# Quantised attention and LoRA feed-forward: quantised x transposed by DMA, and the adapters gated for both batches at once

## The chip, the core and the metric

The kernel runs on one core of a Trainium2 chip. The metric is the device time of one execution in microseconds (us), the median of several runs. The engines are TensorE (PE; its weight loads are listed as PEld), VectorE (DVE), ScalarE (ACT), GpSimd (POOL) and SyncE (SP). In this kernel SP only issues DMA transfers; ScalarE issues some as well, on a queue of its own.

## The reference: what is computed

There are two batches of 1024 tokens with 2048 features each. For each batch:

```
q1 = fake_quant(layernorm(x));  q2 = fake_quant(ctx)      # 8 bits, ctx is 2048 x 2048 per batch
x  = x + q1 @ q2
z  = layernorm(x)
x  = x + z @ kernel + bias + lora(z)
```

The LoRA part sees the 2 x 1024 tokens as 8 groups of 256 tokens. Group b has its own adapter, which is a mixture of 16 adapters of rank 32, weighted by row b of `gate`; beside it there is a shared adapter of rank 32:

```
A_eff = einsum('bn,nri->bri', gate, lora_A)      # per group 32 x 2048
B_eff = einsum('bn,nor->bor', gate, lora_B)
delta = (z @ A_eff.T) @ B_eff.T + (z @ A_shared.T) @ B_shared.T
```

Mixing the adapters by `gate` is called gating below. It does not depend on x.

## The kernel before

The work is done batch by batch. A batch has 8 token tiles of 128 tokens, in 4 groups of 256 (index `g`), and 4 blocks of 512 output columns (index `n`).

**Attention stage.** `prep_x(b, m)` makes one tile of quantised x. VectorE computes statistics (L283 and the small operations after it). ScalarE quantises the tile to 8 bits (L295) and then converts each half of it to bf16 in the buffer `qh` (L298). There is one `qh` for both halves of a tile, and the next tile uses it again; the 8-bit buffer `q8` alternates between two. TensorE transposes the eight 128x128 blocks of a half into PSUM (`pt`, L303), and VectorE copies them to `c1T` (L304), the operand of the attention matmuls.

`quantise` does the same for ctx in pieces of 512 KB: ScalarE writes 16-bit integers (L314) to one of three `q2b` buffers, and VectorE clips and centres them (L317). `column_term` sums the columns of one block of quantised ctx (`pcp` and `pc`). `xattn_pair(b, n, g)` opens the accumulator on ScalarE (L359), runs 2 x 16 matmuls (`pa`, L361), and adds the result to `y` on VectorE (L370).

**Gating.** `load_next` streams ctx and the raw adapters, in an order written out by hand in `todo`, into ten `lit` buffers by DMAs on the SP queue. `gated` multiplies a 256-row slice of raw adapters at a time with `gmat`, a 128 x 32 matrix of gates for the 4 groups of one batch. Four such matmuls fill the four 32-row strips of one PSUM tile (`pg_a` or `pg_b`, L383), which VectorE copies to a `q2b` buffer (L395). For A, `lora_a_step` transposes that tile on TensorE (`pga`, L403) and VectorE sorts it into `acat` (L406). For B, `lora_b_step` writes it to DRAM in eight small DMAs on SP (`bd`, L416), from where `Delta` loads it later. All of it is done once per batch: four A steps and four B steps, set between the attention pairs.

**Feed-forward stage.** `prep_z` normalises and transposes `y` (`ptz`), stores it to DRAM (`zs`) and `lora_ax` applies `acat` (`px`). Then `ffn` runs a two-level Strassen scheme in f32: 7 outer by 7 inner products (L611), with the sums of operands on VectorE and GpSimd (L551, L560), the results added to `y` (L629), and the delta of the adapters slipped in (`pl`, L483). During the last outer product of batch 0, `meanwhile` already prepares batch 1: ctx is quantised and tiles 0 to 3 go through `prep_x`.

The Tile framework places the instructions of each engine in a static order by priorities and dependencies; each engine and each DMA queue then works through its own order and waits where a semaphore tells it to. A DMA also waits for the DMA that used the same completion semaphore before it, and there are eight of these for the SP and ScalarE queues together.

Of the kernel before, what the change touches and what calls it, by code (L numbers as in the profile page):

```python
# [10 lines left out]
F32 = mybir.dt.float32  # L11
# [9 lines left out]
P = 128  # L21
# [45 lines left out]
def tile_quant_xattn_then_lora_ffn(  # L67
# [30 lines left out]
    H = D // 2  # L98
    KH = KT // 2
    KQ = KT // 4  # L100
    GP = GPB * RC

    const = ctx.enter_context(tc.tile_pool(name="const", bufs=1))
    small = ctx.enter_context(tc.tile_pool(name="small", bufs=4))
# [18 lines left out]
    gmat = const.tile([P, 2, GPB // 2, RC], F32, tag="gmat", name="gmat")  # L123
# [7 lines left out]
    ]  # L131


    bd = [dram.tile([GPB, 2, R, D], F32, tag=f"bd{b}", name=f"bd{b}") for b in range(B)]

    def bf(t, n):

# [18 lines left out]
    for b in range(B):  # L156
        for n in range(2):
            todo.extend((b, raw_src(b, n, r)) for r in range(KT // 2))
        for n in range(2, 4):
            for r in range(KT // 2):  # L160
                todo.append((b, raw_src(b, n, r)))
                if r in ((3, 7) if n == 2 else (5, 7)):
                    todo.extend((b, ad_src(la, 2 * (n - 2) + r // 6 if n == 3 else r // 4, h)) for h in range(2))
        for n in range(NN):
            todo.extend((b, ad_src(lb, n, h)) for h in range(2))
    loaded = deque()
    ahead = [2]
# [48 lines left out]

    ident = const.tile([P, P], F32, tag="ident", name="ident")
    make_identity(nc, ident)
    ident_h = const.tile([P, P], BF16, tag="ident_h", name="ident_h")
    nc.gpsimd.tensor_copy(ident_h, ident)  # L220
    ones_h = const.tile([P, P], BF16, tag="ones_h", name="ones_h")
    nc.gpsimd.memset(ones_h, 1.0)

# [22 lines left out]
    for b in range(B):  # L246
        for i in range(2):
            nc.vector.tensor_reduce(
                gval[:, ds(b * GPB + i * 2, 2)], gate_b[:, b * GPB + i : (b + 1) * GPB : 2, :], AX.X, ALU.add
            )  # L250

    def norm_stats(stats, name):
# [22 lines left out]
    def prep_x(b, m, c1T, wk):  # L277

        nm = f"{b}_{m}"
        g, tok = m // MG, ds((m % MG) * P, P)  # L280
        ym = y[g][:, m % MG, :]
        for n in range(NN):
            nc.vector.bn_stats(st1[:, m, n, :], ym[:, ds(n * NB, NB)])  # L283
        mean, rstd = norm_stats(st1[:, m], f"a{nm}")

        k = small.tile([P, 1], F32, tag="kx", name=f"kx_{nm}")
        nc.vector.tensor_mul(k, rstd, inv1)
        o = small.tile([P, 1], F32, tag="ox", name=f"ox_{nm}")
# [6 lines left out]
        nc.scalar.activation(q8, ym, AF.Identity, bias=o, scale=k)  # L295
        rsum = small.tile([P, 2], F32, tag="rsum", name=f"rsum_{nm}")
        for h in range(2):
            nc.scalar.activation(  # L298
                qh[:, ds(h * H, H)], q8[:, ds(h * H, H)], AF.Identity, bias=n_centre, accum_out=rsum[:, h : h + 1]
            )  # L300
            pt = ps_m.tile([P, KH, P], BF16, tag="pm", name=f"pt_{nm}_{h}")
            for kt in range(KH):
                nc.tensor.transpose(pt[:, kt, :], qh[:, ds(h * H + kt * P, P)], ident_h)  # L303
            nc.vector.tensor_copy(c1T[g][:, ds(h * KH, KH), tok], pt)  # L304
# [18 lines left out]

    colt = {}
    pairs = []

    def column_term(b, n, c2):

# [21 lines left out]
    def xattn_pair(b, n, g, c1T, c2):  # L350

        cols = ds(n * NB, NB)
        pairs.append((b, n, g))
        pa = ps_acc.tile([P, MG, NB], F32, tag=("acc0", "acc1", "delta")[len(pairs) % 3], name=f"pa_{b}_{n}_{g}")
        for j in range(MG):

            m = g * MG + j
            with tc.high_priority():
                nc.scalar.activation(pa[:, j, :], colt[n], AF.Identity, bias=r_s[:, m : m + 1])  # L359
            for k in range(KT):  # L360
                nc.tensor.matmul(  # L361
                    pa[:, j, :],
                    c1T[g][:, k, ds(j * P, P)],
                    c2[k // 8][:, k % 8, :],
                    start=False,
                    stop=(k == KT - 1),
                    skip_group_check=True,
                )
        yp = y[g][:, :, cols]
# [6 lines left out]
    def gated(nm):  # L376

        ps = ps_m.tile([P, NB], F32, tag="pm", name=f"pg_{nm}")
        for h in range(2):
            buf, t = next_loaded()  # L380
            for c in range(2):
                row = (2 * h + c) * GP
                nc.tensor.matmul(  # L383
                    ps[row : row + GP, :],
                    gmat.rearrange("p i a r -> p (i a r)"),
                    t[:, c, :],
                    start=True,
                    stop=True,
                    skip_group_check=True,
                )  # L390
            lit.give(buf)
            load_next()
# [3 lines left out]
        return st, sf  # L396

    def lora_a_step(b, n):

        st, sf = gated(f"a{b}_{n}")  # L400
        pt = ps_m.tile([P, KQ, P], F32, tag="pm", name=f"pga_{b}_{n}")
        for k in range(KQ):
            nc.tensor.transpose(pt[:, k, :], sf[:, ds(k * P, P)], ident)  # L403
        q2b.give(st)
        for g in range(GPB):
            nc.vector.tensor_copy(  # L406
                acat[:, ds(n * KQ, KQ), own_col[g], :].rearrange("p k (c r) -> p k c r", c=NC),
                pt.rearrange("p k (c i a r) -> p i a k c r", c=NC, i=2, r=RC)[:, g % 2, g // 2],
            )

    def lora_b_step(b, n):

        st, sf = gated(f"b{b}_{n}")
        for c in range(NC):
            for i in range(2):
                nc.sync.dma_start(  # L416
                    out=bd[b][i::2, i, ds(c * RC, RC), ds(n * NB, NB)],
                    in_=sf[ds(c * GP + i * (GP // 2), GP // 2), :],
                )
        q2b.give(st)  # L420

    def prep_z(b, m, zq, wk):

# [34 lines left out]
    class Delta:  # L458
# [7 lines left out]
        def step(self):  # L466
# [4 lines left out]
            if j == 0:  # L471
                self.bp, self.bb = bp.take(), bias_b.take()
                nc.scalar.dma_start(
                    out=self.bp, in_=bd[self.b][ds(2 * pr, 2), :, :, cols].rearrange("g s r n -> (g s r) n")
                )
                nc.scalar.dma_start(out=self.bb, in_=bias[cols].partition_broadcast(P))
            pl = ps_acc.tile([P, 2, NB], F32, tag="delta", name=f"pl_{self.b}_{n}_{pr}_{j}")
# [213 lines left out]
            big.give(t)  # L691

    for b in range(B):
        nc.vector.tensor_tensor(
            gmat.rearrange("p i a r -> p (i a) r"),
            m_rk.unsqueeze(1).to_broadcast([P, GPB, RC]),
            gval[:, ds(b * GPB, GPB)].unsqueeze(2).to_broadcast([P, GPB, RC]),
            ALU.mult,
        )
        if b == 0:  # L700
            open_c2(0)
            prep_x(0, 0, c1T, wk)
# [21 lines left out]
        for g in range(2, GPB):  # L724
# [3 lines left out]
            for n in range(2):  # L728
                xattn_pair(b, n, g, c1T, c2[n])
                if g + 1 == GPB:  # L730
# [3 lines left out]
                    if n == 0:  # L734
                        for r in range(NR):
                            quantise(c2[2], r)
                            if r % 4 == 3:
                                lora_a_step(b, r // 4)
                        column_term(b, 2, c2[2])
        if b == 0:  # L740
            for pr in range(GPB // 2):
                nc.sync.dma_start(out=acat[:, :, 3 * pr + 1, :], in_=a_sh)
            for bb in range(B):
                for g in range(GPB):
                    nc.sync.dma_start(out=bd[bb][g, 1 - g % 2], in_=b_sh)
        for g in range(GPB):
            xattn_pair(b, 2, g, c1T, c2[2])
            for r in {0: range(3), 1: range(3, 6), 2: range(6, 8), 3: ()}[g]:
                quantise(c2[3], r)
            if 1 <= g <= 2:  # L750
                lora_a_step(b, g + 1)
            if g == 2:
                column_term(b, 3, c2[3])
        lora_b_step(b, 0)
        close_c2(2)
        bp.give(colt.pop(2))
        first = Operands(b, 0)
# [2 lines left out]
        for g in range(GPB):  # L760
# [149 lines left out]
```

## Time and profile before

| | |
|---|---|
| median of 3 runs | 1130.41 us (1127.37 to 1130.59) |
| profiled execution, its own time | 1128.61 us |
| its span | 1126.8 us |
| TensorE busy | 1072.4 us, 95% of the span |
| VectorE busy | 741.5 us, 66% |
| ScalarE busy | 261.1 us, 23% |
| DMA traffic | 261.35 MB, 232 GB/s on average |
| granted TensorE clock | 0.999 |

The span of a profile runs from the first to the last instruction. Two rough maps help in reading the rest. In time, the attention stage of batch 0 takes the first 225 us, its feed-forward stage reaches to about 590 us (the last 45 us overlap with batch 1's preparation), the attention stage of batch 1 follows to about 757 us, and its feed-forward stage ends the span. In rows, a line such as `L303 PE MATMUL pt<-ident_h,big ... x256 | 20.3, 231 | 29.6 <-ACT big L298` says: line 303, on TensorE, writes `pt` from `ident_h` and `big`, 256 instructions that kept the engine busy for 20.3 us in all, 231 ns for one (they overlap), and before them the engine stood idle for 29.6 us, mostly for ScalarE's line 298. "big", "lit" and "q2b" are pools of buffers that hold many things in turn.

### The profile page before, as it was taken

The numbers are of one execution on the slowest core, as the hardware profiler recorded it, in microseconds if no ns is written. First come the engines' busy times: TensorE is split into PE (matmuls) and PEld (weight loads), VectorE is DVE, ScalarE is ACT, GpSimd is POOL, SyncE is SP. The second block draws the span as 40 slices with busy tenths as digits, with TensorE's granted clock in tenths as the row PEclk, the third lists the DMA queues.
The fourth block names the chain that finished last, engine by engine and source line by source line (L and its number), as shares of the span: only waits on it lengthen the run. The fifth ranks groups of instructions, "written<-read, shape, count | busy, mean of one in ns | idle before, by whom it ended". The sixth has DMA issues, their size and how long they took to land.

```text
span 1126.8 us, 10619 instructions
## 1 busy us (share of the span) xinstructions
PE 1072.4 (95%) x3926; PEld 489.3 (43%) x3926; DVE 741.5 (66%) x969; ACT 261.1 (23%) x342; POOL 266.6 (24%) x106
## 2 busy tenths in 40 slices
PE   1689899999999999999999999999999999999998
PEld 0244334554444444444444433455444444444443
DVE  4685547576696768568777654766668586865861
ACT  5875513320001010001375761232000000000000
POOL 0000000234253422525000000022535343243600
PEclk9999999999999999999999999999999999999999
DMA  8991935885789757489857094588668875749611
GB/s 307 391 244 35 282 124 217 298 322 205 246 285 377 266 181 264 141 301 355 285 184 228 1 277 154 182 301 314 244 215 293 295 255 181 256 145 322 213 38 56
DMA packets 120772, 261.35 MB, mean 232 GB/s; under 512 B 11920, under 2 KB 16144, under 8 KB 119568
## 3 DMA queue, kind: packets, MB, share of 16 engines
q1 hardware_dynamic: 99264, 218.65, 56.6%
q10 hardware_dynamic: 21456, 42.02, 10.5%
q8 instruction: 31, 0.51, 0.2%
q14 instruction: 21, 0.17, 0.0%
HBM read 224.99 MB, written 37.75 MB: 233 GB/s over the span
## 4 chain that ended last, share of the span: by engine, by line
PE 80%; DMA 7%; DVE 6%; ACT 4%; issue 1%; SPq 1%; ACTq 0%; DVEq 0%
PE fu L611 33%; PE fv L611 17%; PE pa L361 13%; PE fw L611 9%; DMA lit<-in_ctx_dram 4%; PE pl L483 3%; PE ptz L432 2%; DVE big L560 1%; PE pg_a L383 1%; DVE st L283 1%; PE pg_b L383 1%; ACT big L298 1%; ACT big L295 1%; DMA bd<-q2b 1%; DMA big<-in_w_dram 1%
## 5 line engine op out<-in xcount | busy, mean ns | idle before, releaser
L611 PE MATMUL fu<-big,lit 128*128 128x512 f32 x896 | 396.3, 594 | 2.4 <-DVE y L629 2.4
L560 POOL TENSOR_TENSOR lit<-lit,lit 128x1024 f32<-128x1024 f32 x56 | 165.2, 2957 | 539.4 <-PE pa L361 209.1
L611 PEld LDWEIGHTS fu<-big,lit 128*128 128x128 f32 x896 | 167.8, 190 | 208.2 <-issue 206.7
L361 PE MATMUL pa<-big,big 128*128 128x512 bf16 x1024 | 238.0, 382 | 11.9 <-ACT pa L359 10.6
L611 PE MATMUL fv<-big,lit 128*128 128x512 f32 x448 | 198.1, 594 | 0.0
L551 POOL TENSOR_TENSOR lit<-lit,lit 128x1024 f32<-128x1024 f32 x40 | 100.9, 2524 | 283.4 <-DMA lit<-zs 255.5
L560 DVE TENSOR_TENSOR big<-big,big 128x2048 f32<-128x2048 f32 x56 | 159.4, 2850 | 5.9 <-PE ptz L432 5.3
L361 PEld LDWEIGHTS <-big 128*128 128x128 bf16 x1024 | 97.0, 98 | 146.5 <-issue 44.3
L629 DVE TENSOR_TENSOR y<-y,fu 128x1024 f32<-128x1024 f32 (+1 forms) x98 | 113.7, 1194 | 67.2 <-PE fu L611 66.8
L611 PEld LDWEIGHTS fv<-big,lit 128*128 128x128 f32 x448 | 84.3, 190 | 105.0 <-issue 105.0
L629 DVE TENSOR_TENSOR y<-y,fv 128x1024 f32<-128x1024 f32 x48 | 56.8, 1218 | 91.1 <-PE fv L611 91.1
L478 ACT COPY pl<-bias 128x1024 f32<-128x1024 f32 x32 | 32.6, 1017 | 344.9 <-DVE y L493 327.1
L314 ACT ACTIVATE q2b<-lit,sc,inv 128x1024 int16<-128x1024 f32 x64 | 76.6, 1230 | 146.4 <-DMA lit<-in_ctx_dram 124.7
L551 DVE TENSOR_TENSOR big<-big,big 128x2048 f32<-128x2048 f32 x40 | 101.7, 2544 | 13.2 <-DMA big<-in_w_dram 13.2
L611 PE MATMUL fw<-big,lit 128*128 128x512 f32 x224 | 100.6, 596 | 0.1
L370 DVE SCALAR_TENSOR_TENSOR y<-pa,k_s,y 128x1024 f32<-128x1024 f32 x32 | 41.0, 1282 | 69.7 <-PE pa L361 69.7
L359 ACT ACTIVATE pa<-bp,r_s 128x512 f32<-128x512 f32 x64 | 42.8, 684 | 105.6 <-PE pa L361 60.5
L629 DVE TENSOR_TENSOR y<-y,fw 128x1024 f32<-128x1024 f32 x24 | 28.4, 1217 | 52.5 <-PE fw L611 52.5
L611 PEld LDWEIGHTS fw<-big,lit 128*128 128x128 f32 x224 | 41.3, 190 | 48.7 <-issue 48.2
L303 PE MATMUL pt<-ident_h,big 128*128 128x128 bf16 x256 | 20.3, 231 | 29.6 <-ACT big L298 29.4
L283 DVE BATCH_NORM_STATS2 st<-y 128x6 f32<-128x512 f32 x64 | 42.1, 680 | 2.9 <-DMA y<-in_x_dram 2.9
L317 DVE TENSOR_SCALAR big<-q2b 128x1024 bf16<-128x1024 int16 x64 | 27.6, 440 | 23.7 <-ACT q2b L314 20.5
(79 smaller groups left out, 609.9 us busy)
## 6 DMA issues: line engine op xcount, KB each, us to landing
big<-in_w_dram SPq DMA_DIRECT2D x96, 1024.0 KB
lit<-zs SPq DMA_DIRECT2D x88, 512.0 KB
lit<-in_ctx_dram SPq DMA_DIRECT2D x64, 512.0 KB
out_dram<-y ACTq DMA_DIRECT2D x30, 512.0 KB
zs<-lit ACTq DMA_DIRECT2D x24, 512.0 KB
y<-in_x_dram SPq DMA_DIRECT2D x8, 1024.0 KB
lit<-in_lora_a_dram SPq DMA_DIRECT2D x32, 256.0 KB
lit<-in_lora_bt_dram SPq DMA_DIRECT2D x32, 256.0 KB
```

The source lines that it names most:

```text
L283: nc.vector.bn_stats(st1[:, m, n, :], ym[:, ds(n * NB, NB)])
L314: nc.scalar.activation(qi, t, AF.Relu, bias=z2, scale=inv2)
L317: nc.vector.tensor_scalar(c2[r // 4][:, ds(2 * (r % 4), 2), :], qi, QMAX, CENTRE, ALU.min, ALU.subtract)
L359: nc.scalar.activation(pa[:, j, :], colt[n], AF.Identity, bias=r_s[:, m : m + 1])
L361: nc.tensor.matmul(pa[:, j, :], c1T[g][:, k, ds(j * P, P)], c2[k // 8][:, k % 8, :], start=False, stop=(k == KT - 1), skip_group_check=True,)
L370: summed = nc.vector.scalar_tensor_tensor(yp, pa, s12, yp, ALU.mult, ALU.add)
L478: nc.scalar.copy(pl, self.bb.unsqueeze(1).to_broadcast([P, 2, NB]))
L483: nc.tensor.matmul(pl[:, i, ds(h * (NB // 2), NB // 2)], axT[rows, pr, ds(j * P, P)], self.bp[rows, ds(h * (NB // 2), NB // 2)], start=Fal ...
L551: line(eng.tensor_tensor(got[0], got[0], got[1], ALU.add if terms[1][2] > 0 else ALU.subtract))
L560: line(eng.tensor_tensor(out_t, at[p], at[q], op))
L611: nc.tensor.matmul(ps[:, m, :], at[:, k, ds(m * P, P)], bt[:, k, :], start=(opens and k == 0), stop=(ends and k == KQ - 1), skip_group_che ...
L629: line(nc.vector.tensor_tensor(yp, yp, chains[chain][:, js, :], ALU.add if sign > 0 else ALU.subtract))
```

## The change

There are two parts. First, `prep_x` transposes quantised x by a DMA: after L298 has written a half of `qh`, ScalarE's queue issues one DMA transpose of 128 x 1024 bf16 values from `qh` straight into `c1T`. The TensorE transposes, the VectorE copies and the bf16 identity are gone.

Second, `gmat` holds the gates of all 8 groups (128 x 64), so that one pass over the raw adapters gates them for both batches, all of it in batch 0. `gated` works on one half of a column block: two matmuls of 64 rows each, one copy to `q2b`, and four DMAs on SP that write the result to DRAM, for B to `bd` as before and for A to a new tensor `ad`. Each batch then reads its part of A back by two DMAs on ScalarE's queue (`load_at`), into a `lit` buffer each, and transposes it on TensorE behind a given attention pair (`lora_at_step`), with two copies on VectorE for each column block. Batch 1 no longer loads raw adapters.

```diff
-    GP = GPB * RC
+    GP = GB * RC
...
-    bd = [dram.tile([GPB, 2, R, D], F32, tag=f"bd{b}", name=f"bd{b}") for b in range(B)]
+    ad = dram.tile([2, GB // 2, R, D], F32, tag="ad", name="ad")
+    bd = dram.tile([GB, 2, R, D], F32, tag="bd", name="bd")
...
-                if r in ((3, 7) if n == 2 else (5, 7)):
+                if b == 0 and r in ((3, 7) if n == 2 else (5, 7)):
                     todo.extend((b, ad_src(la, 2 * (n - 2) + r // 6 if n == 3 else r // 4, h)) for h in range(2))
-        for n in range(NN):
+        for n in range(NN if b == 0 else 0):
             todo.extend((b, ad_src(lb, n, h)) for h in range(2))
...
             nc.scalar.activation(
                 qh[:, ds(h * H, H)], q8[:, ds(h * H, H)], AF.Identity, bias=n_centre, accum_out=rsum[:, h : h + 1]
             )
-            pt = ps_m.tile([P, KH, P], BF16, tag="pm", name=f"pt_{nm}_{h}")
-            for kt in range(KH):
-                nc.tensor.transpose(pt[:, kt, :], qh[:, ds(h * H + kt * P, P)], ident_h)
-            nc.vector.tensor_copy(c1T[g][:, ds(h * KH, KH), tok], pt)
+
+            nc.scalar.dma_start_transpose(out=c1T[g][:, ds(h * KH, KH), tok], in_=qh[:, ds(h * H, H)])
...
+    def gated(nm, n, h, dst):
 
         ps = ps_m.tile([P, NB], F32, tag="pm", name=f"pg_{nm}")
+        buf, t = next_loaded()
+        for c in range(2):
+            nc.tensor.matmul(
+                ps[c * GP : (c + 1) * GP, :],
+                gmat.rearrange("p i a r -> p (i a r)"),
+                t[:, c, :],
+                start=True,
+                stop=True,
+                skip_group_check=True,
+            )
+        lit.give(buf)
+        load_next()
         st = q2b.take()
         sf = st.rearrange("p k n -> p (k n)").bitcast(F32)
         nc.vector.tensor_copy(sf, ps)
+        for c in range(2):
             for i in range(2):
                 nc.sync.dma_start(
+                    out=dst[i][:, ds((2 * h + c) * RC, RC), ds(n * NB, NB)],
                     in_=sf[ds(c * GP + i * (GP // 2), GP // 2), :],
                 )
         q2b.give(st)
+
+    def load_at(b, n2):
+
+        buf = lit.take()
+        nc.scalar.dma_start(
+            out=flat(buf),
+            in_=ad[:, ds(b * GPB // 2, GPB // 2), :, ds(2 * n2 * NB, 2 * NB)].rearrange("i a r n -> i (a r) n"),
+        )
+        return buf
+
+    def lora_at_step(b, n2, buf, behind):
+
+        t = flat(buf)
+        for n in range(2):
+            pt = ps_m.tile([P, KQ, P], F32, tag="pm", name=f"pga_{b}_{n2}_{n}")
+            with tc.issue_after(behind):
+                for k in range(KQ):
+                    nc.tensor.transpose(pt[:, k, :], t[:, ds((n * KQ + k) * P, P)], ident)
+            for pr in range(GPB // 2):
+                nc.vector.tensor_copy(
+                    acat[:, ds((2 * n2 + n) * KQ, KQ), 3 * pr : 3 * pr + 3 : 2, :],
+                    pt.rearrange("p k (i a r) -> p a k i r", i=2, r=R)[:, pr],
+                )
+        lit.give(buf)
...
                         for r in range(NR):
                             quantise(c2[2], r)
-                            if r % 4 == 3:
-                                lora_a_step(b, r // 4)
+                            if b == 0 and r % 4 == 3:
+                                lora_a_step(r // 4)
...
-            if 1 <= g <= 2:
-                lora_a_step(b, g + 1)
+            if b == 0 and 1 <= g <= 2:
+                lora_a_step(g + 1)
+            if g == 2:
+                at0 = load_at(b, 0)
             if g == 2:
                 column_term(b, 3, c2[3])
-        lora_b_step(b, 0)
+        lora_at_step(b, 0, at0, last_mm[-1].ins)
+        if b == 0:
+            lora_b_step(0)
...
-            if g < 3:
-                lora_b_step(b, g + 1)
+            if g == 0:
+                at1 = load_at(b, 1)
+            if g == 1:
+                lora_at_step(b, 1, at1, last_mm[-1].ins)
+            if b == 0 and g < 3:
+                lora_b_step(g + 1)
```

More of the change, by code (lines that the diff above doesn't have):

```diff
@@ L122, in tile_quant_xattn_then_lora_ffn @@
     axT = const.tile([P, GPB // 2, GT], F32, tag="axT", name="axT")
-    gmat = const.tile([P, 2, GPB // 2, RC], F32, tag="gmat", name="gmat")
+    gmat = const.tile([P, 2, GB // 2, RC], F32, tag="gmat", name="gmat")
     st1 = const.tile([P, MT, NN, 6], F32, tag="st1", name="st1")
@@ L218, in tile_quant_xattn_then_lora_ffn @@
     make_identity(nc, ident)
-    ident_h = const.tile([P, P], BF16, tag="ident_h", name="ident_h")
-    nc.gpsimd.tensor_copy(ident_h, ident)
     ones_h = const.tile([P, P], BF16, tag="ones_h", name="ones_h")
@@ L245, in tile_quant_xattn_then_lora_ffn @@
     nc.vector.tensor_tensor(gate_b, gate_b, m_ad.unsqueeze(1).to_broadcast([P, GB, NL]), ALU.mult)
[L246 to L250, printed above, removed]
+    for i in range(2):
+        nc.vector.tensor_reduce(gval[:, ds(i * GB // 2, GB // 2)], gate_b[:, i::2, :], AX.X, ALU.add)
+    nc.vector.tensor_tensor(
+        gmat.rearrange("p i a r -> p (i a) r"),
+        m_rk.unsqueeze(1).to_broadcast([P, GB, RC]),
+        gval.unsqueeze(2).to_broadcast([P, GB, RC]),
+        ALU.mult,
+    )
     def norm_stats(stats, name):
@@ L325, in tile_quant_xattn_then_lora_ffn @@
     pairs = []
+    last_mm = []
     def column_term(b, n, c2):
@@ L360, in xattn_pair @@
             for k in range(KT):
-                nc.tensor.matmul(
+                mm = nc.tensor.matmul(
                     pa[:, j, :],
@@ L368, in xattn_pair @@
                 )
+        last_mm.append(mm)
         yp = y[g][:, :, cols]
@@ L373, in xattn_pair @@
         return summed
-    def gated(nm):
+    def gated(nm, n, h, dst):
         ps = ps_m.tile([P, NB], F32, tag="pm", name=f"pg_{nm}")
[L379 to L392, printed above, removed]
+        buf, t = next_loaded()
[10 more added lines that the diff above has]
+        load_next()
         st = q2b.take()
@@ L395, in gated @@
         nc.vector.tensor_copy(sf, ps)
[L396 to L414, printed above, removed]
+        for c in range(2):
             for i in range(2):
                 nc.sync.dma_start(
-                    out=bd[b][i::2, i, ds(c * RC, RC), ds(n * NB, NB)],
+                    out=dst[i][:, ds((2 * h + c) * RC, RC), ds(n * NB, NB)],
                     in_=sf[ds(c * GP + i * (GP // 2), GP // 2), :],
@@ L420, in lora_b_step, with lora_a_step @@
         q2b.give(st)
+    def lora_a_step(n):
+        for h in range(2):
+            gated(f"a_{n}_{h}", n, h, ad)
+    def lora_b_step(n):
+        own = [bd[i::2, i] for i in range(2)]
+        for h in range(2):
+            gated(f"b_{n}_{h}", n, h, own)
+    def load_at(b, n2):
[16 more added lines that the diff above has]
+                    pt.rearrange("p k (i a r) -> p a k i r", i=2, r=R)[:, pr],
+                )
+        lit.give(buf)
     def prep_z(b, m, zq, wk):
@@ L473, in step @@
                 nc.scalar.dma_start(
-                    out=self.bp, in_=bd[self.b][ds(2 * pr, 2), :, :, cols].rearrange("g s r n -> (g s r) n")
+                    out=self.bp, in_=bd[ds(self.b * GPB + 2 * pr, 2), :, :, cols].rearrange("g s r n -> (g s r) n")
                 )
@@ L693, in tile_quant_xattn_then_lora_ffn @@
     for b in range(B):
[L694 to L699, printed above, removed]
         if b == 0:
@@ L742, in tile_quant_xattn_then_lora_ffn @@
                 nc.sync.dma_start(out=acat[:, :, 3 * pr + 1, :], in_=a_sh)
-            for bb in range(B):
-                for g in range(GPB):
-                    nc.sync.dma_start(out=bd[bb][g, 1 - g % 2], in_=b_sh)
+            for g in range(GB):
+                nc.sync.dma_start(out=bd[g, 1 - g % 2], in_=b_sh)
         for g in range(GPB):
```

## The prediction

> **What bounds the kernel now.** I read the busy times first, then the chain of waits, then busy time by stage, then the timelines of TensorE, ScalarE and the SP queue in the attention stages. All from one profiled execution: span 1126.8 us, 1128.61 us in all, 1.8 us below the median of 1130.41. I add differences to the median. About 0.3% (3.4 us) is what a measurement can tell from no change.
>
> ```profile
> PE 1072.4 (95%) x3926; PEld 489.3 (43%) x3926; DVE 741.5 (66%) x969; ACT 261.1 (23%) x342; POOL 266.6 (24%) x106
> ...
> L303 PE MATMUL pt<-ident_h,big 128*128 128x128 bf16 x256 | 20.3, 231 | 29.6 <-ACT big L298 29.4
> ...
> L304 DVE COPY big<-pt 128x1024 bf16<-128x1024 bf16 x32 | 21.2, 682 | 1.1 <-PE pt L303 1.1
> ...
> L383 PE MATMUL pg_a<-lit,gmat 128*32 128x512 f32 x64 | 14.8, 605 | 0.0
> L383 PE MATMUL pg_b<-lit,gmat 128*32 128x512 f32 x64 | 14.8, 605 | 0.0
> ```
>
> TensorE is the bound on average: 20.3 us of it are the transposes of quantised x, 29.6 us the gating matmuls of both batches. The stages differ (columns: length, then busy PE, PEld, DVE, ACT, POOL, clock, DMA share, GB/s):
>
> ```profile
> 0.00:50.00 50.00, 17.68 (x79) 7.58 (x80) 25.66 (x89) 31.52 (x35) 1.25 (x10) 1.00 0.91 349
> 50.00:90.00 40.00, 34.72 (x214) 16.98 (x213) 31.24 (x87) 33.62 (x43) 0.00 (x0) 1.00 0.81 229
> ...
> 545.00:592.00 47.00, 46.16 (x183) 21.33 (x182) 34.74 (x89) 30.15 (x36) 2.35 (x1) 1.00 0.69 223
> ...
> 620.00:660.00 40.00, 39.17 (x232) 17.82 (x230) 26.09 (x66) 28.18 (x35) 0.00 (x0) 1.00 0.27 83
> 660.00:700.00 40.00, 39.91 (x193) 15.73 (x192) 19.24 (x34) 12.50 (x16) 0.00 (x0) 1.00 0.69 189
> ```
>
> Up to about 70 us ScalarE sets the pace (33.6 of 40 us busy; unbroken from 14.7 to 38 us); from about 100 us on, and through batch 1, TensorE does. The change puts work on the first and takes it off the second. Timeline rows (start, length, engine):
>
> ```profile
> 72.93 1.13 ACT L298 ACTIVATE big<-big,n_centre 128x1024 bf16<-128x1024 uint8 x1
> 75.19 2.08 ACT L295 ACTIVATE big<-y,ox,kx 128x2048 uint8<-128x2048 f32 x1
> ...
> 161.86 5.08 SPq L416 DMA_DIRECT2D bd<-q2b  x8
> ...
> 199.67 0.33 ACTq L439 DMA_DIRECT2D zs<-lit  x1
> ...
> 652.29 1.06 PE L383 MATMUL pg_a<-lit,gmat 128*32 128x512 f32 x8
> ```
>
> and from the chain of waits, two landings:
>
> ```profile
> 738.05 5.65 DMA zs<-lit
> ...
> 79.89 4.27 DMA bd<-in_b_sh_dram
> ```
>
> **Price of one DMA transpose.** Thirty-two of them (128x1024 bf16, 256 KB) replace eight TensorE transposes and one VectorE copy each. No row shows one, and two prices matter: h, how long the ScalarE queue is held by the issue, and L, from issue to landing. For h the nearest row, a plain DMA issue on that queue, is 0.33 to 0.41 us: the lower end. For L, plain transfers land in 4.3 us (b_sh) and 5.6 us (zs): I take 5.
>
> [...] Row: eight TensorE transposes run in 0.61 us (79 ns each), the copy in 0.68 us, so a half tile is turned in 1.3 us. [...]
>
> **The sum, stage by stage.** `prep_x` writes one half-tile buffer pair `qh`, used again by the next tile: its L298 now waits for the previous tile's landing, and ScalarE runs in order, so quantise (L314) and the opening of accumulators (L359) queue behind that wait, and matmuls behind them.
>
> *0 to 42 us.* Four transposes stand in ScalarE's unbroken run: 4 x 1.5 = +6. The next tile's L298 comes some 8 us later: no landing wait. Two of VectorE's copies leave the path to `pcp`: -1. Net +5.
>
> *42 to 70 us.* Tiles 2 and 3: +6 of issue, and tile 3 waits 5 less its cover (one L359 0.67, one issue 1.5, one L314 1.24): +1.6. ScalarE idles 5.3 us here (1.93, 1.29, 2.04), partly in waits for VectorE that move along; half covers: +4 to +5. I take +4.
>
> *70 to 105 us.* Tiles 4 to 7: 12 of issue. In the built order tiles 5 and 7 have an L295 (2.08) and two L359 before the reuse: 5 - 3.4 = 1.6 each. Tile 6 has one short L359: 4.1. Together 19.3 against ScalarE idle of some 13 us (2.0, 0.4, 0.5, 4.4, 2.8, 3.2): +6. TensorE no longer runs 4.6 us of `pt`, but it waits for landings: I credit 1. Net +5.
>
> *105 to 225 us.* Gating for both batches has 64 columns a matmul, so two fit side by side instead of four. The rows show a pair split over two slots takes 1.0 + 1.0 us and all four together 1.06: two halves take 2 us per column block, and six of batch 0's eight steps already did. Under +2, taken 0. A goes out by 32 new SP issues (64 KB each). They hold two of the three `q2b` buffers until they land, and quantise shares these: four steps then run ScalarE-to-VectorE in series, about 2.1 instead of 1.23 us each, +3.5. On SP they cost 32 x 0.57 to 0.65 (0.65 is 5.08/8), some 20 us, ahead of ctx and adapter loads queued behind them, each A write itself waiting for VectorE's copy. Cover: c2[3]'s last ctx was quantised at 130 us and wanted at 152 by `pcp`, and SP idled from 142 to 158. I take +0.5; without that cover it costs the rest, to +10. Reading A back (`load_at`, on ScalarE's queue) waits for those writes; issued one pair (some 9 us) ahead of the transposes, it fits a landing of 5: 0, or up to +4 if late. The 32 `pga` transposes stay; their 32 copies (0.28) become 16 larger ones: 0. Net +4.
>
> *545 to 592 us.* Eight transposes, 12 us, into 17 us of ScalarE slack; TensorE loses four tiles of `pt`, 4.4 us; the last landing comes at about the time the second pair needs it: +2. Net -2.
>
> *592 to 644 us.* As at 70 to 105: 19.3 against about 19 idle. But the chain ran ScalarE to TensorE here (L298 at 618 and 634, `pa` next): tile 4's 1.9 us of `pt` and copy become two issues and a landing, 8, exposed +6, tile 6 partly, +3; TensorE gives back 4.6. Net +5.
>
> *644 to 735 us.* All gating of batch 1 goes: 8 steps x 1.85 = 14.8 us of bound TensorE. Late next: `c2[2]` can't be quantised before its buffers come free at 644, and eight L314 (1.23) plus `pcp` end near 658 as now, so most of the 4.1 us of `pg_a` before 656 turns into waiting: -12. SP loses 32 adapter loads and 32 writes; w is loaded earlier, but TensorE was hardly waiting: 0, or down to -4.
>
> *FFN loops.* Nothing moves: 0.
>
> Sum: 5 + 4 + 5 + 4 - 2 + 5 - 12 = +9, so 1139 or 1140.
>
> **Rivals.**
> *Cheap transposes (ends faster).* One mechanism: the issue costs like a plain one (0.4) and landings hide. Then the stages give +1, 0, -3, +4, -4, -2, -12: -16, 1114. For: the plain rows, and DMA idle in 620 to 660 us (share 0.27). Against: the DMA share of 0.91 at the start, where landings queue. All else fixed, the thirty-two issues weigh about 22 us between h = 0.4 and 1.5 and the landings the rest; the change of sign lies at h near 1 us.
> [...]
> *A's round trip dominates.* Transposes are as in my sum, but A writes behind loads starve `q2b` and delay c2[3] past 152 us: +10 to +15 more, 1150 to 1155. For: SP waits in the trace of 14.9 us each for L416 behind w loads and zs stores. Against: 22 us of cover.
> That gating isn't halved (no gain in batch 1) is excluded by the code: no adapter load or gating stands in batch 1.
>
> **How the numbers follow.** My sum 0.42 (1127 to 1150, of this 0.05 within 0.3% and nothing faster), cheap 0.26 (0.24 faster, 0.02 within), crossbar-bound 0.20, A's round trip 0.12. Faster 0.24, same 0.07, slower 0.69. The range 1112 to 1178 leaves out the lower edge of the cheap case and the upper half of the crossbar case. Likeliest 1140.
>
> **What would show it.** Right: no `pt` rows; a DMA-transpose row on ScalarE's queue of about 1.5 us; first `pa` near 47 us instead of 42; pair (0,0,2) late by some 10 us; `pg_b` gone after 600 us; batch 1's stretch from 592 to the first `fu` shorter by 5 to 10 us. Wrong, cheap: issue under 0.6 us and L298 never waiting on a DMA. [...] A's trip: L314 waiting on `ad` writes around 105 to 130 us, or `pcp` late at 152.

## The result, and the profile after

| | before | after |
|---|---|---|
| median | 1128.95 us of 4 runs (1127.37 to 1130.59) | 1168.24 us of 4 runs (1159.03 to 1171.63) |
| ratio after to before | | 1.0335, 95% interval 1.0273 to 1.0397 |
| profiled execution | 1128.61 us, span 1126.8, clock 0.999 | 1159.03 us, span 1157.0, clock 0.991 |

The change makes the kernel 3.3% slower: 39 us, where the sum had 9 or 10. The profiled execution of after is the fastest of its four; the other three took 1167.45 to 1171.63 us at granted clocks of 0.981 to 0.983. What the trace can account for is therefore 30 us; the other 9 stay open. The lower clock by itself does not explain them: of 41 executions of the kernel before (those beside runs 5 to 8 below), the 15 at a granted clock of 0.982 to 0.985 took 1128.5 us on average, the 26 at 0.994 to 1.000 took 1129.0.

The page of after, first its busy times, then three rows of its DMA issues:

```profile
PE 1060.9 (92%) x3580; PEld 478.5 (41%) x3606; DVE 721.8 (62%) x918; ACT 262.7 (23%) x342; POOL 263.5 (23%) x105
...
ad<-q2b SPq DMA_DIRECT2D x32, 64.0 KB
...
lit<-ad ACTq DMA_DIRECT2D x4, 512.0 KB
...
big<-big ACTq DMA_TRANSPOSE x32
```

The new work is the 32 writes of A, their 4 reads, and 32 DMA transposes. The old work is gone as announced: TensorE is busy 11.5 us less and VectorE 19.7 us less, yet the span is 30 us longer. TensorE's share fell from 95 to 92%: the loss is waiting. The groups of the gating matmuls, shapes kept apart, show the other half of the bargain:

```profile
L382 PE MATMUL pg_a<-lit,gmat 128*64 128x512 f32 x32 | 10.3, 614 | 0.0
L382 PE MATMUL pg_b<-lit,gmat 128*64 128x512 f32 x32 | 9.7, 635 | 6.0 <-DVE q2b L394 5.1 <-PE pa L361 0.8
```

Half as many matmuls, 20.0 us for 29.6 before, since two fit side by side now and not four: four of them take 1.08 us (at 114.3 us), where eight took 1.06. All 20.0 are in batch 0 now, which had 14.8. Note the new idle time before `pg_b`, put down to the copy L394: it leads to the main loss.

The same stages as before by windows, those of batch 1 moved along by 36 us (columns: length, then busy PE, PEld, DVE, ACT, POOL, clock, DMA share, GB/s):

```profile
0.00:50.00 50.00, 10.03 (x28) 2.29 (x29) 21.55 (x77) 24.42 (x27) 1.02 (x9) 1.00 0.87 287
50.00:90.00 40.00, 29.81 (x123) 11.60 (x121) 22.49 (x69) 29.39 (x36) 0.00 (x0) 1.00 0.97 301
581.00:628.00 47.00, 46.89 (x129) 19.84 (x129) 32.08 (x80) 24.34 (x28) 2.36 (x1) 1.00 0.90 258
656.00:696.00 40.00, 37.16 (x173) 16.00 (x176) 21.15 (x54) 31.03 (x39) 0.00 (x0) 1.00 0.41 93
```

In the first window ScalarE computes for 24.4 us where it had 31.5, though its work is the same: the transposes hold its queue. The last two are batch 1, which did about what was expected. The landmarks below (starts of instructions in TensorE's timeline) put the loss in its place:

| | before | after | later by |
|---|---|---|---|
| first `pa`, batch 0 | 42.3 | 52.3 | 10.0 |
| `pc` of `c2[1]` | 64.3 | 77.9 | 13.6 |
| `pc` of `c2[2]` | 118.2 | 134.1 | 15.8 |
| `pc` of `c2[3]` | 154.1 | 167.4 | 13.3 |
| first `px` | 202.3 | 239.1 | 36.8 |
| second `px` | 232.6 | 272.7 | 40.1 |
| first `pa`, batch 1 | 590.0 | 626.1 | 36.1 |
| second `px`, batch 1 | 771.2 | 802.1 | 30.8 |
| span | 1126.8 | 1157.0 | 30.2 |

Two steps make the loss: about 14 us in the first 80, and about 24 between 167 and 240 us. Batch 1 gives 9 back. The first step, in ScalarE's timeline (start, length, and in brackets the idle time before a row):

```profile
23.39 1.34 ACTq L303 DMA_TRANSPOSE big<-big  x1
...
24.77 5.65 ACTq L303 DMA_TRANSPOSE big<-big  x1
30.47 1.24 ACT L313 ACTIVATE q2b<-lit,sc,inv 128x1024 int16<-128x1024 f32 x1 [5.98 <-issue]
...
38.34 1.42 ACTq L303 DMA_TRANSPOSE big<-big  x1
...
39.80 4.51 ACTq L303 DMA_TRANSPOSE big<-big  x1
44.36 3.50 ACT L313 ACTIVATE q2b<-lit,sc,inv 128x1024 int16<-128x1024 f32 x3 [4.92 <-issue]
```

The four transposes of tiles 0 and 1 hold the queue for 12.9 us, and `quantise` (L313) stands behind them. The answer for line 303 gives all 32 (minimum, median and maximum in ns, then who waited for the landings):

```profile
L303 ACTq DMA_TRANSPOSE big<-big x32: 1247/1282/5651, 23.4 to 682.9; - x32
...
  PE pa L361: 6.3, 4
  ACT big L299: 1.0, 2
```

The second step begins with `load_at`. Rows of the timelines of ScalarE, TensorE, SP and VectorE:

```profile
161.36 1.12 ACTq L417 DMA_DIRECT2D lit<-ad  x1
...
174.46 1.06 PE L430 MATMUL pga<-ident,lit 128*128 128x128 f32 x8 [2.54 <-DMA lit<-ad]
...
174.39 3.85 SPq L180 DMA_DIRECT2D lit<-in_lora_bt_dram  x6
178.33 5.17 SPq L397 DMA_DIRECT2D ad<-q2b  x8
...
185.49 0.69 DVE L394 COPY q2b<-pg_b 128x512 f32<-128x512 f32 x1 [7.76 <-DMA ad<-q2b]
...
186.23 1.97 PE L382 MATMUL pg_b<-lit,gmat 128*64 128x512 f32 x2 [5.07 <-DVE q2b L394]
188.13 4.64 PE L361 MATMUL pa<-big,big 128*128 128x512 bf16 x16
...
206.68 1.38 PE L430 MATMUL pga<-ident,lit 128*128 128x128 f32 x8 [4.31 <-DMA lit<-ad]
```

Of the waits of SP's queue between 100 and 260 us, those for A's reads (total, times, longest):

```profile
...
SPq L557 <- DMA lit<-ad: 14.1, 1, 14.1
SPq L180 <- DMA lit<-ad: 13.1, 1, 13.1
```

and busy time by windows:

```profile
170.00:176.00 6.00, 3.46 (x20) 1.90 (x19) 2.16 (x3) 1.34 (x3) 0.00 (x0) 1.00 0.11 39
182.00:188.00 6.00, 1.77 (x2) 0.29 (x2) 0.69 (x1) 0.00 (x0) 0.00 (x0) 0.62 0.24 88
188.00:194.00 6.00, 6.00 (x22) 2.19 (x22) 1.88 (x2) 0.00 (x0) 0.00 (x0) 0.82 0.37 113
```

The first read of A is issued at 161.4 us and lands at 174.3: 13 us for 512 KB, while the DMA engines are busy to a share of 0.11 and move 39 GB/s (170 to 176 us). Two engines of 16 would be 0.125. The packets of ScalarE's queue between 161 and 174.4 us, 130 of them with 0.52 MB, take 9.8% of the time of 16 engines, which is 1.6 engines' worth. The slowest dimension of `ad[:, ...]` is `i`, of size 2. That this shape kept the read to about two engines was my estimate; runs 3 and 4 try another shape. The trace records each increment of a completion semaphore: the first read has three, one 1.2 us after its issue and two more at 12.7 and 13.0 us, and the other three reads have three as well, where each of the 32 transposes has 16.

Then the queues pass it on. SP waits 13.1 us for this read and 14.1 for the second. What waits has no use for the data: the first time it is a load of raw adapters (L180), the second time a load of w (L557). In the trace, where eight semaphores tell of the landings of both queues, each of these loads is the next transfer on the semaphore of the read before it, so the wait is for the shared completion semaphore. When the first read has landed, six adapter loads go out, and behind them, at 178.3 us, eight A writes. VectorE's copy L394 waits 7.8 us for a `q2b` buffer that those writes still read. TensorE's next `pg_b` waits 5.07 us for that copy to empty a PSUM tile, and the attention matmuls stand behind it. In 182 to 188 us TensorE works for 1.8 of 6 us, and it comes back slowly: 16 `pa` take 4.64 us, 290 ns each, at a granted clock of 0.82 (undisturbed they take 3.63). The granted clock is 1.00 in the window from 170 us, 0.62 in the one with the stall and 0.82 in the next. The second read can go out only at 188.0 us, when the last of the A writes has landed; it takes until 206.5 us (4.31 us before `pga` at 206.7), and a w load stands behind it.

### The profile page after: what moved, and what is told of

It is laid out like the page before. It is cut to its first block, busy times and chain, and to the rows that moved or that the text cites. A ratio compares the mean times of both kernels' runs of the same rounds, so it can differ in the third digit from the quotient of the medians.

```text
span 1157.0 us, 9893 instructions
## 1 busy us (share of the span) xinstructions
PE 1060.9 (92%) x3580; PEld 478.5 (41%) x3606; DVE 721.8 (62%) x918; ACT 262.7 (23%) x342; POOL 263.5 (23%) x105
## 5 line engine op out<-in xcount | busy, mean ns | idle before, releaser
L576 POOL TENSOR_TENSOR lit<-lit,lit 128x1024 f32<-128x1024 f32 x56 | 162.6, 2911 | 564.9 <-DMA zs<-lit 247.2
L567 POOL TENSOR_TENSOR lit<-lit,lit 128x1024 f32<-128x1024 f32 x40 | 100.5, 2514 | 291.0 <-DMA lit<-zs 234.1
L361 PEld LDWEIGHTS <-big 128*128 128x128 bf16 x1024 | 99.6, 99 | 154.5 <-issue 42.9
L576 DVE TENSOR_TENSOR big<-big,big 128x2048 f32<-128x2048 f32 x56 | 157.9, 2822 | 5.5 <-PE ptz L448 5.0
L313 ACT ACTIVATE q2b<-lit,sc,inv 128x1024 int16<-128x1024 f32 x64 | 76.4, 1231 | 166.9 <-DMA lit<-in_ctx_dram 120.3
L567 DVE TENSOR_TENSOR big<-big,big 128x2048 f32<-128x2048 f32 x40 | 100.4, 2510 | 15.4 <-DMA big<-in_w_dram 15.4
L333 PE MATMUL pcp<-big,ones_h 128*32 128x512 bf16 x128 | 17.7, 420 | 41.6 <-DVE big L316 41.5
L444 DVE TENSOR_SCALAR big<-y,mv_z,rstd_z 128x1024 f32<-128x1024 f32 x32 | 29.1, 935 | 25.6 <-PE ptz L448 25.5
```

The source lines that it names most:

```text
L313: nc.scalar.activation(qi, t, AF.Relu, bias=z2, scale=inv2)
L333: nc.tensor.matmul(parts[row : row + P // 4, :], ones_h[:, 0 : P // 4], c2[k // 8][:, k % 8, :], start=(k < 4), stop=(k >= KT - 4), skip_g ...
L361: mm = nc.tensor.matmul(pa[:, j, :], c1T[g][:, k, ds(j * P, P)], c2[k // 8][:, k % 8, :], start=False, stop=(k == KT - 1), skip_group_chec ...
L444: nc.vector.tensor_scalar(t, y[g][:, m % MG, ds(h * H, H)], mean, rstd, ALU.subtract, ALU.mult)
L567: line(eng.tensor_tensor(got[0], got[0], got[1], ALU.add if terms[1][2] > 0 else ALU.subtract))
L576: line(eng.tensor_tensor(out_t, at[p], at[q], op))
```

## The experiments

All times are against the kernel before, run beside them on the same chip (medians 1128.5 to 1129.1 us). The landmarks are from the profiled executions, and differences of 5 us between single profiles are within what executions of these kernels differ by. The profiles of runs 2, 4 and 5 are the slowest executions of their kernels, 6.5, 4.9 and 3.5 us over the medians, so that their delays are rather too large; that of after is its fastest.

**1. Transposes alone.** The kernel before with the edit in `prep_x` and nothing of the gating.

> The kernel before with the DMA transposes alone; gating stays once per batch. Theory T (transposes hold ScalarE early on: the changed kernel's summed delay at the column term of c2[2] in batch 0 was 15.8 us, nearly all before any A write): this kernel carries most of those 15.8 us to its end, gets back some 5 us of pt work in batch 1, and none of the gating: 1138 to 1150 us. Theory G (the gating part is what costs): under 1134 us.

**2. Gating alone.** After, with the TensorE transposes put back:

```diff
-            nc.scalar.dma_start_transpose(out=c1T[g][:, ds(h * KH, KH), tok], in_=qh[:, ds(h * H, H)])
+            pt = ps_m.tile([P, KH, P], BF16, tag="pm", name=f"pt_{nm}_{h}")
+            for kt in range(KH):
+                nc.tensor.transpose(pt[:, kt, :], qh[:, ds(h * H + kt * P, P)], ident_h)
+            nc.vector.tensor_copy(c1T[g][:, ds(h * KH, KH), tok], pt)
```

> The kernel before with gating for both batches and A through DRAM alone; x is still transposed on TensorE. Theory G (the read of A back lands late and holds SP, q2b and TensorE, about 20 us between 154 and 202 us of the span, given back by 12 to 15 us in batch 1): 1130 to 1142 us. Theory T: the transposes are the whole loss and this part is a gain: 1112 to 1120 us.

**3 and 4. A's read in two transfers.** In after (3) and in gating alone (4), `load_at` reads each `i` by a DMA of its own, so that the slowest dimension is 64 rows on both sides:

```diff
-        nc.scalar.dma_start(
-            out=flat(buf),
-            in_=ad[:, ds(b * GPB // 2, GPB // 2), :, ds(2 * n2 * NB, 2 * NB)].rearrange("i a r n -> i (a r) n"),
-        )
+        for i in range(2):
+            nc.scalar.dma_start(
+                out=flat(buf)[ds(i * P // 2, P // 2), :],
+                in_=ad[i, ds(b * GPB // 2, GPB // 2), :, ds(2 * n2 * NB, 2 * NB)].rearrange("a r n -> (a r) n"),
+            )
```

> The changed kernel with each read of A split in two DMAs of 64 partitions, whose slowest dimension is then 64 rows instead of 2. If the read is slow because one DMA with a slowest dimension of 2 runs on two DMA engines (landing 13 us with a DMA share of 0.11 to 0.22), landing falls to 4 to 6 us, SP's 13 and 14 us waits on it go, and the whole falls by 12 to 25 us, to 1143 to 1156. If the delay is q2b starvation by the A writes, or the small writes themselves, it falls by under 5 us.

> Gating for both batches alone (TensorE transposes kept), with the split read. If the two-engine read is what turned this part into a loss, this is faster than the kernel before by 8 to 15 us (1114 to 1121). If the A writes on SP and in q2b are the cost, it stays within 5 us of the kernel before.

Measured, with the landmarks as delays against before:

| | median us | ratio (95%) | `pc` of `c2[2]` | first `px` | second `px` | second `px`, batch 1 |
|---|---|---|---|---|---|---|
| after | 1168.24 | 1.0335 (1.0273 to 1.0397) | 15.8 | 36.8 | 40.1 | 30.8 |
| 1, transposes alone | 1142.38 | 1.0117 (1.0102 to 1.0132) | 18.1 | 16.2 | 16.7 | 14.0 |
| 2, gating alone | 1147.31 | 1.0170 (1.0139 to 1.0201) | 7.4 | 33.0 | 33.9 | 25.8 |
| 3, after, read split | 1157.29 | 1.0266 (1.0228 to 1.0304) | 23.4 | 30.6 | 37.2 | 27.5 |
| 4, gating, read split | 1132.11 | 1.0033 (1.0018 to 1.0048) | 5.3 | 14.3 | 17.2 | 9.1 |

Run 1 puts the first step on the transposes: all of their delay is there by 118 us, and none is added up to the second `px`. Run 2 puts the second step on the gating: 26 us between `c2[2]` and the first `px`. It was larger than I expected. SP's waits in run 2, 150 to 200 us, and those of the other engines:

```profile
SPq L180 <- DMA lit<-ad: 14.4, 1, 14.4
SPq L401 <- DMA lit<-ad: 13.8, 1, 13.8
```

```profile
ACT pa L363 <- DMA bd<-q2b: 14.0, 1, 14.0
PE pga L434 <- DMA lit<-ad: 8.9, 2, 6.1
```

SP stands 14.4 and 13.8 us for A's read. ScalarE's opening of an accumulator (L363) is 14.0 us late as well, put down to a write of `bd`. But it stands behind the second `load_at` in ScalarE's order, and that one waits for the last writes of A, which SP could issue only after its 14.4 us. Rows of SP's timeline and ScalarE's:

```profile
170.96 5.08 SPq L401 DMA_DIRECT2D ad<-q2b  x8
...
179.87 0.53 ACTq L421 DMA_DIRECT2D lit<-ad  x1
```

The split undoes most of it: run 4 is 15.2 us faster than run 2. Run 2's two reads in batch 0 land 16.1 and 17.4 us after their issue; in run 4 each half has 16 increments of its semaphore, not three, and lands after 5.6 to 8.0 us. So it is the shape that made the read slow. A read now holds SP for 4.6 us at most (SP's waits in run 4):

```profile
SPq L180 <- DMA lit<-ad: 4.6, 1, 4.6
```

The split gave after less than I expected (11.0 us, for 12 to 25), and run 4 did not come out under before (1114 to 1121 hoped for): in batch 1 it returns 7.9 of the 14.8 us of gating matmuls, but it enters batch 1 17 us late. What holds it then, in VectorE's waits, 150 to 200 us, and in its timeline and TensorE's:

```profile
DVE q2b L398 <- DMA bd<-q2b: 7.5, 1, 7.5
```

```profile
179.15 0.69 DVE L398 COPY q2b<-pg_b 128x512 f32<-128x512 f32 x1 [7.47 <-DMA bd<-q2b]
...
183.71 5.30 PE L365 MATMUL pa<-big,big 128*128 128x512 bf16 x16 [4.06 <-ACT pa L363]
```

The chain is much as in after, but it starts with the small writes rather than with the read: there are three `q2b` buffers, each held until its writes have landed, and the sum into `y` and the next accumulator wait behind L398. The TensorE stall is 4.06 us, and the next 16 `pa` take 5.30. The writes have a short slowest dimension too, the 4 groups of one `i`: in run 4 each write of A has five increments, and its 64 KB take 2.9 to 5.8 us. No run gave them another shape.

**5 and 6. The buffers, and the queue of the writes.** Run 5 is run 4 with a fourth `q2b`, lent from `axT` (not yet in use) until batch 0's last B step; run 6 is run 4 with the writes on GpSimd's queue instead of SP's.

```diff
+    spare4 = axT.rearrange("p a t -> p (a t)").bitcast(I16).rearrange("p (k n) -> p k n", k=2)
+    q2b.give(spare4)
...
+            if b == 0 and g == 2:
+                q2b.spare = deque(t for t in q2b.spare if t is not spare4)
```

```diff
-                nc.sync.dma_start(
+                nc.gpsimd.dma_start(
```

> Gating for both batches with the split read and TensorE transposes, and a fourth q2b buffer (the space of axT, lent until the last B step of batch 0). In the run with three buffers VectorE's copy of a gating result waited 7.5 us for a buffer held by B writes, and the sum into y, the next accumulator and the matmuls waited behind it (4.1 us on TensorE, and a lowered clock after it). If q2b starvation is what keeps this part from gaining, 1120 to 1127 us. If the queueing of the writes on SP is the cause, a fourth buffer fills up as well and it stays at 1129 to 1133.

> The same gating kernel with three q2b buffers, its small writes of A and B issued from GpSimd's queue, so that they wait neither behind w loads nor ahead of adapter loads. If SP's order is the cause: 1118 to 1126 us. If the landing of the writes themselves holds q2b: no better than 1130; worse if GpSimd's issue is slow, up to 1136.

Run 5: 1130.90 us (20 runs), ratio 1.0016 (1.0005 to 1.0027). The wait of L398 for writes is gone, the first `px` is 7.4 us late instead of 14.3, but the second is 14.1 us late. The waits of run 5, 150 to 240 us:

```profile
ACT axT L479 <- DMA zs<-lit: 7.8, 1, 7.8
...
PE ptz L455 <- ACT axT L479: 4.1, 1, 4.1
```

The wait has moved: ScalarE now stands for a `zs` store of `prep_z`, and TensorE for ScalarE. What makes that store late was not separated. Run 6: 1142.57 us, ratio 1.0122 (1.0091 to 1.0153), slower than run 4 by 10 us: now quantise waits for the A writes. They go out at about the same times as in run 4 (110 to 166 us, there 109 to 165), but land after 5.4 us in the median, for 4.1 there (ScalarE's waits in run 6):

```profile
ACT q2b L317 <- DMA ad<-q2b: 15.6, 4, 6.3
```

So getting the writes off SP's queue does not free the ring of `q2b` earlier; on GpSimd's it is freed later.

**7. Transposes from SP's queue.** Run 1 with `nc.sync.dma_start_transpose`.

> The kernel before with DMA transposes alone, issued from SP's queue instead of ScalarE's. If the hold of ScalarE's queue (1.25 us each, up to 5.65 us at a DMA share of 0.9) is what delays the first attention matmul from 42.3 to 52.5 us, it comes back to 42 to 45 us, while ctx loads queue behind transposes that wait for L298 on SP: 1132 to 1140 us. If contention in the DMA engines is the cause and not the queue's place, the first matmul stays at 50 us or later and the time at 1140 or above.

1136.74 us, ratio 1.0063 (1.0043 to 1.0082), 5.6 us under run 1. The first `pa` starts at 38.0 us, earlier than before the change (42.3): with the issue off ScalarE, turning x by DMA does shorten the way to it. The hold moves to SP, whose timeline has

```profile
23.46 7.94 SPq L300 DMA_TRANSPOSE big<-big  x2
31.46 2.14 SPq L176 DMA_DIRECT2D lit<-in_ctx_dram  x4
...
56.06 11.18 SPq L300 DMA_TRANSPOSE big<-big  x2
```

two transposes for 7.9 and 11.2 us, with the ctx loads behind them, and L296 waits 8.6 us in all for landings, where after's L299 waited 1.0. By `c2[2]` it is 6.0 us late.

**8. Transposes in batch 1 alone.** Run 1 with batch 0 on TensorE.

> The kernel before with DMA transposes for batch 1 alone; batch 0 keeps TensorE. If only the start of the kernel pays for the transposes, this gains: TensorE loses 10 us of pt work, most of it under full load, some given back in waits for ScalarE: 1124 to 1128 us. If the hold of ScalarE costs as much in batch 1 as TensorE gains, within 0.3% of 1129.

1125.88 us (20 runs), ratio 0.9973 (0.9964 to 0.9983): the only version here that is under the kernel before, by 0.27%. The answer for its transposes, and two of its stages:

```profile
L302 ACTq DMA_TRANSPOSE big<-big x16: 1247/1260/3051, 565.3 to 643.1; - x16
```

```profile
545.00:592.00 47.00, 46.54 (x136) 19.64 (x136) 29.65 (x78) 27.57 (x34) 2.35 (x1) 1.00 0.88 252
592.00:610.00 18.00, 13.74 (x64) 4.99 (x64) 13.21 (x22) 12.16 (x12) 0.00 (x0) 1.00 1.07 299
```

Between 545 and 592 us TensorE is the bound and is rid of four tiles of `pt`: the first `pa` of batch 1 comes 3.7 us earlier (586.3). Right behind, in 592 to 610, it is idle for 4.3 of 18 us, the DMA share at 1.07. From there to the second `px` of batch 1 it takes 183.8 us for 181.3. In the profile the net is 1.1 us, in the medians 2.9.

**9 and 10. Together.** Run 9 is run 5 with the transposes of run 8; run 10 is after with the split read and the fourth `q2b`.

> Gating for both batches with A's read in two transfers and a fourth q2b lent until batch 0's last B step (the kernel that measured 1130.9), and in addition the DMA transposes in batch 1 alone (which by themselves measured 1125.9, 3 us under the kernel before). Additive theory: the two parts touch different stretches, so 1130.9 - 3 = 1128 (1125 to 1131), and the first px of batch 0 stays near 210 us. Rival, no addition: with the gating of batch 1 gone, TensorE has no slack left between 604 and 640 us in which the transposes' 15 to 20 us until the first pcp are hidden, so batch 1 loses what it gave back: 1133 to 1140.

> The changed kernel with A's read in two transfers of 64 partitions and a fourth q2b lent until batch 0's last B step. Theory, the gating's parts add to the transposes': e1 was +13 over before and gating with these two mends +2, so 1129 + 13 + 2 = 1144 (1140 to 1149). Rival, interaction: the late start (first pa near 52 us) leaves the adapters' transfers and the ring still in step with the loads, so that px of batch 0 comes near 230 us as in the split kernel alone and the time stays at 1152 to 1158.

Run 9: 1130.82 us (20 runs), ratio 1.0020 (1.0009 to 1.0030), at the upper end of what addition allows and no better than run 5: the 3 us of run 8 are not to be seen in the median. In the profile its two stretches still gain, 3.9 us up to the first `pa` of batch 1 and 1.3 lost behind it, against run 5. Run 10: 1150.24 us, ratio 1.0189 (1.0172 to 1.0207), between the two theories. Up to the second `px` its delay of 29.0 us is close to the sum of runs 1 and 5 (16.7 + 14.1), so batch 0 adds up; in batch 1 it does not, in this run. From the first `pa` to `pc` of `c2[2]` batch 1 takes 68.2 us before, 69.3 in run 1, 64.5 in run 5, 69.0 in after and 70.0 in run 10. The 4 us that the gating saves there are lost again when the transposes are in. Up to the second `px`, though, after and run 3 still gain 5.3 and 5.6 us, near the 6.3 of runs 1 and 5 together, and only run 10 no more than 2.2. Why was not found.

## Why the prediction was right, and where not

Its direction and its mechanism for the transposes held. That the time lies in its range is luck: the range went up to 1178 us for the crossbar case, which did not come true, while its own sum ended at 1150 us, and the read of A, whose slowness fills most of the gap, was given 4 us at most. Its sum was 29 us short of the median and 21 of the profile; step by step:

*0 to 105 us, forecast +14.* (ScalarE's run in before was read as unbroken from 14.7 to 38 us; it has a gap of 0.56 us and ends at 36.9.) Measured +15.8 at `c2[2]` in after, and +18.1, +23.4 and +19.8 in the profiles of runs 1, 3 and 10, which start alike. The size is near, the parts are not. The hold went into the sum as h = 1.5 us, which no run shows; in its place the issues of after took 1.25 to 5.65 us, 1.28 in the median. It is 1.25 to 1.30 at the end of batch 1's transposes, where the DMA share is 0.41, but 5.65 and 4.51 us for the second half of tiles 0 and 1, where the DMA share is 0.87: 12.9 us for the four, forecast 6. So the first `pa` comes at 52, not at 47. In exchange the landings cost ScalarE next to nothing: L299 waits 1.0 us in all, where I had 8.9 up to 105 us (three times 1.6, and 4.1). They fall on TensorE: `pa` waits 6.3 us for transposed tiles, in four places, and what that does differs. TensorE's timeline in after, and then in run 3:

```profile
65.23 3.63 PE L361 MATMUL pa<-big,big 128*128 128x512 bf16 x16 [2.57 <-DMA big<-big]
72.19 3.63 PE L361 MATMUL pa<-big,big 128*128 128x512 bf16 x16 [3.01 <-DMA big<-big]
```

```profile
65.43 3.63 PE L361 MATMUL pa<-big,big 128*128 128x512 bf16 x16 [2.48 <-DMA big<-big]
75.24 6.51 PE L361 MATMUL pa<-big,big 128*128 128x512 bf16 x16 [5.86 <-DMA big<-big]
```

Behind waits up to 3.0 us 16 `pa` take 3.63 us here, behind one of 5.86 they take 6.51. So one landing that is 3 us later costs `c2[1]` another 6 us (83.8 for 77.9). The length of the wait alone does not decide it. The same wait of 2.15 us, first in before and then in run 2:

```profile
67.50 3.83 PE L361 MATMUL pa<-big,big 128*128 128x512 bf16 x17 [2.15 <-ACT pa L359]
```

```profile
67.28 5.52 PE L365 MATMUL pa<-big,big 128*128 128x512 bf16 x17 [2.15 <-ACT pa L363]
```

The granted clock between 66 and 70 us is 1.00 in the first and 0.67 in the second, so the same wait stands beside either clock; what lowered it was not found.

*105 to 225 us, forecast +4, measured about 24.* This is the term that failed, and in it "`load_at`: 0, or up to +4 if late". I took the landing of a plain transfer, 5 us, for a read with another shape; it took 13.0 and 18.6. The step's own consequence, TensorE late at `pga`, is 6.8 us for both reads. Much of the rest came by the queues, which I had priced for the writes and not for the read: SP stood behind the shared completion semaphore, and with it loads, A writes, `q2b`, L394 and TensorE. Run 4 against run 2 gives this item 15 us. The small writes and the three `q2b`, +3.5 and +0.5 in the sum, have a part in the rest: the fourth buffer takes 7 us off the first `px`, but 3 off the second and only 1 off the median. The matmuls have a part as well, priced "under +2, taken 0": before, batch 0's gating keeps TensorE busy for 14.8 us (half of the 29.6), after for 20.0, and in runs 4 and 5 for 20.6 and 19.9. What each is worth was not separated.

*A's round trip as a rival* had the right stretch and the wrong leg: it named the writes, starving `q2b` before `c2[3]`. In after `c2[3]` is 13.3 us late, less than `c2[2]`; the stall comes behind it, and the read starts it. Its 1150 to 1155 came from 10 to 15 us more; the item was 20 more.

*545 to 592 us, forecast -2.* From the second `px` to batch 1's first `pa`, after takes 353.4 us for 357.3: -3.9. Run 8 shows it alone: -3.7.

*592 us to batch 1's `px`, forecast +5 and -12.* Measured -5.3 in after (176.0 us from the first `pa` to the second `px`, for 181.3). Run 1 has +1.3 (forecast +5), run 5 has -7.6 (forecast -12). Both were sized too far from zero, and the errors nearly cancel.

*FFN loops, forecast 0.* From the second `px` of batch 1 to the end, 355.0 for 355.6.

*Cheap transposes* needed h near 0.4; the shortest is 1.25 us. *Crossbar-bound*, given 0.20, was the case of landings slow throughout; the figure it took for them no run shows. By the increments of the semaphores, the 32 transposes of after land 3.0 to 10.3 us after their issue: 8.2 to 10.3 for tiles 0 and 1, 3.0 to 5.1 for the other six of batch 0, 3.1 to 7.4 in batch 1. L is no constant, as my 5 was: it fits tiles 2 to 5 (3.8 to 5.1 us), and in runs 1, 3 and 10 the half tiles for which TensorE waits longest land after 8.8, 8.2 and 8.3 us, all in the start, at a DMA share of 0.98 to 0.99 between 60 and 90 us.

What stays open is the last 9 us between the profiled execution of after and its median, and why the medians of runs 1 and 4, 13 and 3 us over before, make 16 where run 3 has 28. A start like that of run 3 would give some 6 us: the three profiles in which `pa` waits 4.7 to 5.9 us for a landing (runs 1, 3 and 10) have `pc` of `c2[1]` at 81.8 to 84.1 us and a clock of 0.83 to 0.89 between 60 and 90 us, after has 77.9 and 1.00. But the other three executions of after have no trace, so this is argued, not shown.

## What to carry to other kernels

Write down the shape of both sides of every DMA, not only its bytes: here a read of 512 KB with a slowest dimension of 2 landed after 13.0 and 18.6 us, and splitting it by hand into two, of 64 rows each, was worth 11 to 15 us. A slow transfer that nobody seemed to wait for held those behind it, on both queues here, by a shared semaphore (13.1 and 14.1 us of SP in after) or by an engine that works in order (14.0 us of ScalarE in run 2); price that before its landing. A DMA transpose paid where the engine that it relieves was the bound and the one that issues it had time (batch 1 of run 8, TensorE busy for 46.5 of 47 us and ScalarE for 27.6: -3 us, not seen again beside the new gating), not at a start where that engine set the pace (+14 to +20 us by the first 85 us from ScalarE's queue; from SP's, -5 at that point and +6 by `c2[2]`).

## What was not expected of the hardware

- A transfer of 512 KB with a slowest dimension of 2, and three semaphore increments: 13.0 us at a DMA share of 0.16 (161 to 174 us), 18.6 us at 0.53 with w loads beside it (188 to 206 us). As two transfers with 64 rows as the slowest dimension it landed in 5.6 to 8.0 us in batch 0 of run 4 (run 2: 16.1 and 17.4), and SP's longest wait for it fell from 14.4 to 4.6 us.
- The issue of a DMA transpose held its queue: 1.25 to 1.30 us at a DMA share of 0.41, up to 5.65 us on ScalarE's queue at 0.87, and 11.2 us for two on SP's. A busy stretch is not enough: between 88 and 92 us of after, at a share of 1.21, two issues held it for 1.25 us each. What sets the hold stays open.
- A TensorE stall was paid twice: 16 `pa` behind waits of 4.06 and 5.86 us take 5.30 and 6.51 us, undisturbed 3.63. It is the granted clock that tells, not the length: behind the same wait of 2.15 us, 17 `pa` took 3.83 us at a clock of 1.00 and 5.52 at 0.67.
- From issue to landing a DMA transpose of 128 x 1024 values took 3.0 us at the least, and 8.2 to 10.3 us under the loads of the start (tiles 0 and 1 of after, DMA share 0.87).
